# Shorter expert blocks under two conditions in a row, and a hint for each branch on the way to the next block

## The chip, the cores and the metric

The kernel runs on one core of one Trainium2 chip. The metric is the device time of one execution in microseconds (us); of several runs the median is taken. One of the executions was also recorded by the hardware profiler, and everything said about single instructions comes from that record. The core has five engines that each run their own instruction stream: TensorE (PE, matrix products, with the weight loads listed apart as PEld), VectorE (DVE), ScalarE (ACT), GpSimd (POOL) and SyncE (SP, which here only issues transfers). [...]

## The reference

The network has two layers over 1250 tokens (nodes) of 512 features: in each a graph part, an attention-like mixer and a feed-forward part with a router. The change touches only the last stage, the feed-forward part of the second layer: a layer norm, a router that picks two of eight experts for every token, an expert of 512 to 2048 to 512 with an exact GELU between, and the sum of the two experts' results weighted by their gates.

```python
    def _L1_ffn_ref(x, ln_g, ln_b, w_r, b_r, W1, b1, W2, b2):
        E = 8
        K = 2
        ...
        logits = jnp.einsum('btd,ed->bte', h, w_r) + b_r
        topk_vals, topk_idx = jax.lax.top_k(logits, K)
        gates = jax.nn.softmax(topk_vals, axis=-1)
        hf = h.reshape(B * T, d)
        hid = jax.nn.gelu(jnp.einsum('nd,edf->nef', hf, W1) + b1, approximate=False)
        expert_stack = jnp.einsum('nef,efd->ned', hid, W2) + b2
        ...
        mixed = jnp.sum(gathered * gates_flat[:, :, None], axis=1).reshape(B, T, d)
        return x + mixed
    ...
    x = x + _L1_ffn_ref(_layernorm(x, axis=-1)[None], ...)[0]
```

The reference computes every expert for every token and gathers afterwards. The kernel computes only the pairs of token and expert that the router picked, 2500 of them, so how much work each expert has is known only once the router's result is there.

## The kernel before, in words

**Before the experts.** The graph parts, the mixers, the first layer's feed-forward part and the second router take the first 830 us or so. At their end the kernel has sorted the 2500 pairs by expert, has turned the tokens' features into columns in that order (`hts`, 128 features x slots, four chunks of features), and holds for each slot the row of the output that it belongs to (`to_row`) and its gate (`to_gate`). A small table `plan` says for each expert where its slots start (`first`), how many blocks of 256 slots it fills (`full`), what is left over beside them (`part`: 0 for nothing, 1 for a block of 128, 2 for a block of 192) and its first column in `to_row` and `to_gate` (`col`).

**One block.** `block` (from L1355) runs an expert on 128, 192 or 256 slots. `hidden` makes the 16 chunks (`FC`) of the hidden layer: for each chunk four matmuls (L1306, weights `w1s`, one for each chunk of features) and a GELU on ACT (L1309) that writes `hid[f]`. For 128 and 256 slots `result` follows: for each 128 slots 16 matmuls with `hid[f]` as the weights and `w2s` as the moving data (L1329, 512 columns), one for the bias (L1331), and then `add_rows`: DVE scales by the gates (L1318) and POOL issues an indirect transfer that adds the rows into the output (L1319). For 192 slots `result_192` computes the transposed product, four chunks `c` of 16 matmuls of 192 columns each (L1344, bias L1346), copied out by DVE and turned back by eight transposes (L1352). The data of these matmuls is 32 bits wide, and each stands in the trace as two instructions (32 rows of L1329 for the 16, 0.43 us apart at full clock), the transposes as one.

**The order of the experts.** A Python loop over the eight experts writes the program for all of them out. In it, for expert e: `load_weights` makes SP issue weights of a later expert; `plan_of(e + 1)` loads the next expert's four numbers into registers of every engine (L1386), one expert ahead; then come the conditions, each a compare-and-branch on every engine: is there a shorter block (`part > 0`, L1399); is it 128 wide (`part == 1`, L1400, label `one{e}`), with the 192-wide block as its Else; then the blocks of 256, up to five (`MB`), nested into one another (L1366, label `full{e}_{b}`: is `full > b`).

**What each branch jumps over.** Code is laid out with the "true" arm behind the branch (`preferred_fallthrough_block`), so a true condition goes straight on, and a false one jumps past the block: past 268 recorded matmuls and as many weight loads for a 192-wide one, 161 for a 128-wide one, 194 for each of the five nested blocks of 256. After a 128-wide block there is a jump, without a condition, past the Else, the 192-wide block; it has L1400 as its line. Where a path skips a block, its arm holds the semaphore updates and waits which keep the engines' counts the same on both paths.

**Hints.** `mark_branch_hint_location` puts an instruction into TensorE's stream that tells its sequencer, ahead of a labelled branch, which way it will go; the value is computed in registers (one for "goes straight on", zero for "jumps"). There are two to each block, made by the function `ahead_of` and placed among the last matmuls of the block: in `result` at the last 128 slots' f = 10 and f = 13 (L1327, L1328), in `result_192` at the last chunk's f = 0 and f = 8 (L1342, L1343). The first hints the next L1366 of the same expert, the second the next expert's L1400. L1399 has no hint, and none of the other engines gets any.

**This data.** The router's result for these inputs gives the following blocks in order: expert 0: 128; expert 1: 192; expert 2: 128; expert 3: 192, 256; expert 4: 256; expert 5: 128, 256, 256; expert 6: 192; expert 7: 128, 256, 256, 256. This is read off the widths of TensorE's matmuls in the trace.

SP's order in this stage is written out by hand (`manual_schedule`): its weight loads stand where the loop puts them.

Of the kernel before, what the change touches and what calls it, by code (L numbers as in the profile page):

```python
# [23 lines left out]
DC = D // 128  # L24
# [18 lines left out]
FC = F1 // 128  # L43
FG = F1 // D
NB = (2 * N + 127) // 128
MB = (N + 63) // 256
# [24 lines left out]
def gps_two_layer_kernel(ctx: ExitStack, tc: tile.TileContext, x, src, dst, ew, rows, cols,  # L71
# [1053 lines left out]
    with tc.tile_pool(name="moe", bufs=1) as ep:  # L1125
# [171 lines left out]
        with tc.tile_pool(name="ox", bufs=3) as ox, \  # L1297
# [24 lines left out]
            def result(e, col, width, ahead):  # L1322

                for s in range(width // 128):
                    pm = po.tile([128, D], F32, name="po")
                    for f in range(FC):
                        if s == width // 128 - 1 and f in (FC - 6, FC - 3):  # L1327
                            ahead(f == FC - 6)  # L1328
                        nc.tensor.matmul(pm, hid[f][:, s * 128:(s + 1) * 128], w2s[e, f // DC][:, f % DC, :],  # L1329
                                         start=(f == 0), stop=False)  # L1330
                    nc.tensor.matmul(pm, row_pick[:, e:e + 1].to_broadcast([96, 128]), b2_parts,  # L1331
                                     start=False, stop=True)
                    add_rows(pm, col + s, 128)

            def result_192(e, col, ahead):

                turned = ox.tile([128, DC, 192], F32, name="turned", bufs=1)
                for c in range(DC):
                    pm = po.tile([128, D], F32, name="po")
                    chunk = slice(c * 128, (c + 1) * 128)  # L1340
                    for f in range(FC):
                        if c == DC - 1 and f in (0, FC // 2):  # L1342
                            ahead(f == 0)  # L1343
                        nc.tensor.matmul(pm[:, :192], w2s[e, f // DC][:, f % DC, chunk], hid[f][:, :192],  # L1344
                                         start=(f == 0), stop=False)
                    nc.tensor.matmul(pm[:, :192], b2_parts[:, chunk], row_pick[:, e:e + 1].to_broadcast([96, 192]),  # L1346
                                     start=False, stop=True)
                    nc.vector.tensor_copy(turned[:, c, :], pm[:, :192])
                for s, n in ((0, 128), (1, 64)):
                    pr = po.tile([128, D], F32, name="po")  # L1350
                    for c in range(DC):
                        nc.tensor.transpose(pr[:n, c * 128:(c + 1) * 128], turned[:, c, s * 128:s * 128 + n], ident)  # L1352
                    add_rows(pr, col + s, n)
# [18 lines left out]

                tc.mark_branch_hint_location(f"full{e}_{b}", (plan_e[1] + (7 - b)) // 8, [mybir.EngineType.PE])

            def ahead_of(e, plan_e, b):

                def hint(first):
                    if first and b < MB:
                        fetch_ahead(e, plan_e, b)
                    elif not first and e + 1 in plans:  # L1380
                        tc.mark_branch_hint_location(f"one{e + 1}", (3 - plans[e + 1][2]) // 2,
                                                     [mybir.EngineType.PE])
                return hint

            def plan_of(e):
# [6 lines left out]
            with tc.manual_schedule(engines={mybir.EngineType.SP}):  # L1392
                plans = {0: plan_of(0)}
                for e in range(E1):
                    load_weights(2 * FG * (e + 2))
                    plan_e = plans.pop(e)
                    if e + 1 < E1:
                        plans[e + 1] = plan_of(e + 1)
                    with tc.If(plan_e[2] > 0, preferred_fallthrough_block=True):  # L1399
                        with tc.If(plan_e[2] == 1, label=f"one{e}", preferred_fallthrough_block=True) as one:  # L1400
                            block(e, plan_e, plan_e[1], 128, ahead_of(e, plan_e, 0))
                        with one.Else():
                            block(e, plan_e, plan_e[1], 192, ahead_of(e, plan_e, 0))
                    blocks_of_256(e, plan_e, 0)

# [46 lines left out]
```

## Time and profile before

| what | value |
|---|---|
| runs of the kernel before | median 1511.21 us, 3 runs, 1510.18 to 1511.75 |
| the profiled execution | 1508.84 us, of it 1507.1 us span from first to last instruction |
| mean granted TensorE clock over the span | 0.966 |
| TensorE busy, 0 to 830 us | 750.25 us of 830 |
| TensorE busy, 830 to 1045 us | 200.43 us of 215 |
| TensorE busy, 1045 to 1260 us | 204.08 us of 215 |
| TensorE busy, 1260 to 1500 us | 237.70 us of 240 |
| DVE, ACT, POOL busy, 830 to 1500 us | 25.0, 110.3, 35.6 us |
| instructions fetched for TensorE over the span (queue q8) | 82 packets, 1.34 MB |

The 830 us and the other limits are cuts for the table, near the start of the experts and between two blocks. The experts' stage lasts from there to about 1500 us, and in it the other engines are idle most of the time. The biggest groups of TensorE in it, with busy time, mean duration of one, and the idle time before them with what ended it (`big` and `w` are names of the same weight buffers, pooled):

```profile
L1329 PE MATMUL po<-w,big 128*128 128x512 f32 x576 | 250.1, 592 | 0.0
L1306 PE MATMUL pm<-hts,big 128*128 x960 | 183.3, 353 | 14.8 <-issue 13.5 <-DVE o L1318 1.0 <-PE po L1352 0.3
L1306 PE MATMUL pm<-hts,w 128*128 x832 | 143.5, 334 | 13.8 <-PEq L1399 5.9 <-issue 5.7 <-DMA big<-in_w_dram 2.2
```

"Issue" is time in which the engine waited for nothing that the profile shows, and "PEq" is TensorE's sequencer. All idle time of the two groups of L1306 together is 28.6 us, and it lies in front of the first matmul of a block.

The sequencer's records can be listed by line as well: a compare-and-branch, a load of registers or a semaphore wait with its start and duration. A branch that goes wrong for the instruction fetch shows as one that lasts microseconds.

### The profile page before, as it was taken

What the parts mean: (1) busy time and instruction counts of PE and PEld (TensorE: products, weight loads), DVE (VectorE), ACT (ScalarE), POOL (GpSimd) and SP (SyncE); (2) the same over time, 40 slices, a digit from 0 to 9 for tenths busy, and PEclk for the clock granted to TensorE, in tenths of its full rate; (3) what the DMA queues carried; (4) which work ended last, traced back from release to release, by engine and by line L of the source; (5) the groups of instructions that cost most, each with busy time, mean ns of one, the idle gap of its engine ahead of it and who ended that gap; (6) DMA issues with size and microseconds to landing.
All of it is one profiled execution on the core that took longest, in us unless ns stands there. A gap on an engine that the chain in (4) does not pass through costs nothing. (4 is left out here: it accounts for less than half of the span.)

```text
span 1507.1 us, 18469 instructions
## 1 busy us (share of the span) xinstructions
PE 1392.5 (92%) x6082; PEld 871.0 (58%) x6082; DVE 586.0 (39%) x1425; ACT 404.9 (27%) x937; POOL 199.3 (13%) x176
## 2 busy tenths in 40 slices
PE   5999999999999699999965899899999999999997
PEld 3444445434554346554544697794767577975673
DVE  8887777699775673344476000000000000000000
ACT  8655445301223413112223221210212012110110
POOL 3345445400000000000005000000000000000000
PEclk9999999999999899999986999899999999999999
DMA  7312111522510030001149466600643006101011
GB/s 225 99 55 62 56 55 49 178 83 89 172 48 14 31 131 3 0 1 36 47 152 349 149 222 236 227 9 11 230 125 115 13 3 215 36 6 14 1 14 15
DMA packets 72766, 134.75 MB, mean 89 GB/s; under 512 B 8328, under 2 KB 9720, under 8 KB 72622
## 3 DMA queue, kind: packets, MB, share of 16 engines
q1 hardware_dynamic: 67694, 122.47, 24.0%
q0 software_dynamic: 4928, 10.43, 3.5%
q8 instruction: 82, 1.34, 0.4%
q14 instruction: 62, 0.51, 0.1%
HBM read 107.27 MB, written 26.38 MB: 89 GB/s over the span
## 5 line engine op out<-in xcount | busy, mean ns | idle before, releaser
L1329 PE MATMUL po<-w,big 128*128 128x512 f32 x576 | 250.1, 592 | 0.0
L1306 PE MATMUL pm<-hts,big 128*128 x960 | 183.3, 353 | 14.8 <-issue 13.5
L1318 DVE TENSOR_SCALAR o<-po,to_gate 128x512 f32<-128x512 f32 (+1 forms) x24 | 17.7, 749 | 452.9 <-PE po L1331 451.6
L1306 PEld LDWEIGHTS pm<-hts,big 128*128 128x128 f32 x960 | 165.8, 194 | 34.4 <-issue 19.0
L1329 PEld LDWEIGHTS po<-w,big 128*128 128x128 f32 x576 | 109.1, 190 | 132.1 <-issue 131.5
L1309 ACT ACTIVATE big<-pm,cols_sb 128x256 f32<-128x256 f32 (+2 forms) x224 | 96.2, 433 | 282.5 <-PE pm L1306 281.8
L1306 PE MATMUL pm<-hts,w 128*128 x832 | 143.5, 334 | 13.8 <-PEq L1399 5.9
L1306 PEld LDWEIGHTS pm<-hts,w 128*128 128x128 f32 x832 | 132.1, 197 | 24.6 <-issue 15.6
L455 PE MATMUL pm<-big,ht 128*125 128x512 f32 x240 | 130.9, 633 | 0.0
L1319 POOL DMA_INDIRECT out_dram<-o,row x24 | 37.0, 1540 | 645.2 <-DVE o L1318 284.2
L429 DVE TENSOR_TENSOR at<-at,pa 128x160 f32 x320 | 102.2, 319 | 41.3 <-PE pa L427 17.7
L400 POOL TENSOR_TENSOR hm<-hm,w_low 125x640 bf16<-125x640 bf16 x80 | 100.4, 1276 | 114.0 <-DVE hm L394 63.3
L123 PE MATMUL pm<-w,at 128*125 128x512 f32 x240 | 114.2, 598 | 0.0
L397 ACT ACTIVATE hm<-hm,w_top 125x80 bf16<-125x80 bf16 x320 | 86.4, 350 | 68.1 <-DVE hm L394 55.1
L633 PE MATMUL pn<-big,at 125*125 125x512 f32 x200 | 89.5, 605 | 3.0 <-DMA big<-q_d 3.0
L455 PE MATMUL pm<-big,xt 128*125 128x512 f32 x160 | 88.8, 646 | 1.2 <-DMA x_t<-in_x_dram 1.2
L1309 ACT ACT_TABLE_LOAD x11 | 14.1, 1283 | 248.9 <-PE pm L1306 248.9
L427 PEld LDWEIGHTS <-hs 125*128 125x128 bf16 x640 | 50.8, 97 | 48.8 <-issue 44.0
L424 PE MATMUL pa<-hm,hs 125*128 125x160 bf16 x320 | 64.6, 233 | 13.0 <-DVE at L429 10.9
L424 PEld LDWEIGHTS <-hs 125*128 125x128 bf16 x320 | 31.1, 97 | 67.8 <-issue 38.6
L633 PEld LDWEIGHTS pn<-big,at 125*125 125x125 f32 x200 | 37.5, 190 | 52.7 <-issue 52.7
L427 PE MATMUL pa<-hm,hs 125*128 125x80 bf16 x640 | 64.4, 198 | 0.0
(391 smaller groups left out, 1622.2 us busy)
## 6 DMA issues: line engine op xcount, KB each, us to landing
w<-in_w_dram SPq DMA_DIRECT2D x52, 1024.0 KB
big<-in_w_dram SPq DMA_DIRECT2D x12, 1024.0 KB
x_t<-in_x_dram SPq DMA_DIRECT2D x10, 224.0 KB
xn_d<-xr SPq DMA_DIRECT2D x10, 224.0 KB
y_d<-o SPq DMA_DIRECT2D x10, 224.0 KB
z_d<-o SPq DMA_DIRECT2D x10, 224.0 KB
q_d<-o SPq DMA_DIRECT2D x10, 224.0 KB
k_d<-o SPq DMA_DIRECT2D x10, 224.0 KB
```

Source lines behind the costliest of these rows:

```text
L123: nc.tensor.matmul(ps, lhs[:, c, :], w[:, c, :], start=(c == 0), stop=(row is None and c == DC - 1))
L397: nc.scalar.activation(hm[:, j, 1, :], hm[:, j, 0, :], AF.Copy, scale=w_top[:, g * J + j:g * J + j + 1])
L400: nc.gpsimd.tensor_tensor(hm[:, :, 2 + i, :], hm[:, :, 0, :], w_low[:, i, c8, None].to_broadcast([CH, J, TW]), ALU.mult)
L424: nc.tensor.matmul(pa.rearrange("p k c -> p (k c)"), hs[:, j, :], hm[:, j, 0:2, :].rearrange("p k c -> p (k c)"), start=True, stop=False)
L427: nc.tensor.matmul(pa[:, 1, :], hs[:, j, :], hm[:, j, 2 + i, :], start=False, stop=(i == 1))
L429: add = nc.vector.tensor_tensor(to, to, pa.rearrange("p k (t w) -> p k t w", t=T), ALU.add)
L455: nc.tensor.matmul(pm, lhs[:, c, :], w_sb[:, c, :], start=(c == 0), stop=(row is None and c == DC - 1))
L633: nc.tensor.matmul(pn, at[:P, 0, s, t * P:(t + 1) * P], y[:, s, :], start=(s == 0), stop=(s == T - 1))
L1306: nc.tensor.matmul(pm[:, :width], w1s[e, f // DC][:, c, (f % DC) * 128:(f % DC + 1) * 128], hts[:, c, bass.ds(start, width)], start=(c == ...
L1309: nc.scalar.activation(hid[f][:, :width], pm[:, :width], AF.Gelu, bias=cols_sb[:, C_B11 + e * FC + f:C_B11 + e * FC + f + 1])
L1319: nc.gpsimd.indirect_dma_start(out, bass.IndirectOffsetOnAxis(ap=row[:n], axis=0), o[:n], None, bounds_check=N - 1, oob_is_err=False, comp ...
L1329: nc.tensor.matmul(pm, hid[f][:, s * 128:(s + 1) * 128], w2s[e, f // DC][:, f % DC, :], start=(f == 0), stop=False)
```

## The change

In place of a condition with an Else there are two conditions one after the other, `part == 1` (label `one{e}`) and `part == 2` (label `two{e}`), both inside `part > 0`, which gets the label `any{e}`. After a 128-wide block the jump past the 192-wide one becomes the second condition, false in that case. Up to four hints go into each block in place of two, in the order of the branches that follow: `two` of the same expert (only in a 128-wide block), the next L1366, the next expert's `any`, the next expert's `one`. They stand at f = 10, 11, 12 and 13 of the last 128 slots in `result`, and at f = 0, 2, 4 and 6 of the last chunk in `result_192`. So the hint on L1366 moves by one f in the first and by two in the second, the hint on `one` stays at f = 13 in the first and moves from f = 8 to f = 6 in the second. What is computed stays the same. In the text of the prediction the lines keep their numbers of before; in the changed kernel the load of the plan is L1393, `any` L1406, `one` L1407, `two` L1409, and L1366 stays.

```diff
--- before.py
+++ after.py
@@ -1324,8 +1324,8 @@
                 for s in range(width // 128):
                     pm = po.tile([128, D], F32, name="po")
                     for f in range(FC):
-                        if s == width // 128 - 1 and f in (FC - 6, FC - 3):
-                            ahead(f == FC - 6)
+                        if s == width // 128 - 1 and f >= FC - 6:
+                            ahead(f - FC + 6)
                         nc.tensor.matmul(pm, hid[f][:, s * 128:(s + 1) * 128], w2s[e, f // DC][:, f % DC, :],
                                          start=(f == 0), stop=False)
                     nc.tensor.matmul(pm, row_pick[:, e:e + 1].to_broadcast([96, 128]), b2_parts,
@@ -1339,8 +1339,8 @@
                     pm = po.tile([128, D], F32, name="po")
                     chunk = slice(c * 128, (c + 1) * 128)
                     for f in range(FC):
-                        if c == DC - 1 and f in (0, FC // 2):
-                            ahead(f == 0)
+                        if c == DC - 1 and f % 2 == 0:
+                            ahead(f // 2)
                         nc.tensor.matmul(pm[:, :192], w2s[e, f // DC][:, f % DC, chunk], hid[f][:, :192],
                                          start=(f == 0), stop=False)
                     nc.tensor.matmul(pm[:, :192], b2_parts[:, chunk], row_pick[:, e:e + 1].to_broadcast([96, 192]),
@@ -1372,14 +1372,21 @@
 
                 tc.mark_branch_hint_location(f"full{e}_{b}", (plan_e[1] + (7 - b)) // 8, [mybir.EngineType.PE])
 
-            def ahead_of(e, plan_e, b):
-
-                def hint(first):
-                    if first and b < MB:
+            def ahead_of(e, plan_e, b, shorter=False):
+
+                on_pe = [mybir.EngineType.PE]
+
+                def hint(i):
+                    if i == 0 and shorter:
+                        tc.mark_branch_hint_location(f"two{e}", (plan_e[2] + 1) // 3, on_pe)
+                    elif i == 1 and b < MB:
                         fetch_ahead(e, plan_e, b)
-                    elif not first and e + 1 in plans:
-                        tc.mark_branch_hint_location(f"one{e + 1}", (3 - plans[e + 1][2]) // 2,
-                                                     [mybir.EngineType.PE])
+                    elif i in (2, 3) and e + 1 in plans:
+                        part = plans[e + 1][2]
+                        if i == 2:
+                            tc.mark_branch_hint_location(f"any{e + 1}", (part + 1) // 2, on_pe)
+                        else:
+                            tc.mark_branch_hint_location(f"one{e + 1}", (3 - part) // 2, on_pe)
                 return hint
 
             def plan_of(e):
@@ -1396,10 +1403,10 @@
                     plan_e = plans.pop(e)
                     if e + 1 < E1:
                         plans[e + 1] = plan_of(e + 1)
-                    with tc.If(plan_e[2] > 0, preferred_fallthrough_block=True):
-                        with tc.If(plan_e[2] == 1, label=f"one{e}", preferred_fallthrough_block=True) as one:
-                            block(e, plan_e, plan_e[1], 128, ahead_of(e, plan_e, 0))
-                        with one.Else():
+                    with tc.If(plan_e[2] > 0, label=f"any{e}", preferred_fallthrough_block=True):
+                        with tc.If(plan_e[2] == 1, label=f"one{e}", preferred_fallthrough_block=True):
+                            block(e, plan_e, plan_e[1], 128, ahead_of(e, plan_e, 0, True))
+                        with tc.If(plan_e[2] == 2, label=f"two{e}", preferred_fallthrough_block=True):
                             block(e, plan_e, plan_e[1], 192, ahead_of(e, plan_e, 0))
                     blocks_of_256(e, plan_e, 0)
```

## The prediction

> **What bounds the kernel now.** I read first the page's shares, then TensorE's timeline from 780 us on, then the sequencer's own records, line by line. TensorE is the bound:
>
> ```profile
> span 1507.1 us, 18469 instructions
> PE 1392.5 (92%) x6082; PEld 871.0 (58%) x6082; DVE 586.0 (39%) x1425; ACT 404.9 (27%) x937; POOL 199.3 (13%) x176
> ```
>
> The change touches only the experts, where TensorE stands still between blocks and hardly ever inside one. So the timeline's rows with a bracket (idle time before the row) are what can be won; the two rows without one, at 1145.37 and 1331.97, follow a 128-wide block with no idle time, and these are what can be lost:
>
> ```profile
> 865.21 17.52 PE L1306 MATMUL pm<-hts,big 128*128 x96 [4.19 <-issue]
> ...
> 912.35 16.16 PE L1306 MATMUL pm<-hts,w 128*128 x128 [2.20 <-DMA big<-in_w_dram]
> ...
> 949.47 18.44 PE L1306 MATMUL pm<-hts,big 128*128 x96 [7.01 <-issue]
> ...
> 1057.31 29.47 PE L1306 MATMUL pm<-hts,w 128*128 x128 [5.92 <-PEq L1399]
> ...
> 1145.37 20.88 PE L1306 MATMUL pm<-hts,big 128*128 x96
> ...
> 1259.30 21.06 PE L1306 MATMUL pm<-hts,w 128*128 x128 [2.70 <-issue]
> ...
> 1303.62 10.98 PE L1306 MATMUL pm<-hts,big 128*128 x96 [1.03 <-DVE o L1318]
> ...
> 1331.97 20.88 PE L1306 MATMUL pm<-hts,big 128*128 x96
> ```
>
> The sequencer's records (count: shortest/median/longest ns, first and last start) say what fills a gap. L1400 holds the jump that leaves a shorter block and the condition "is it 128 wide"; L1366 is "another block of 256", L1399 "any shorter block", L1386 the load of the plan:
>
> ```profile
> L1400 PEldq COMPARE_BRANCH  x1: 3372/3372/3372, 853.4 to 853.4; - x1
> L1366 PEldq COMPARE_BRANCH  x1: 4699/4699/4699, 856.8 to 856.8; - x1
> L1400 PEldq COMPARE_BRANCH  x1: 1772/1772/1772, 863.0 to 863.0; - x1
> L1366 PEldq COMPARE_BRANCH  x1: 3330/3330/3330, 1043.7 to 1043.7; - x1
> L1366 PEldq EVENT_SEMAPHORE  x1: 51/51/51, 1051.4 to 1051.4; - x1
> L1386 PEldq TENSOR_LOAD <-plan x1: 997/997/997, 1051.9 to 1051.9; - x1
> L1399 PEldq COMPARE_BRANCH  x1: 3532/3532/3532, 1053.0 to 1053.0; - x1
> L1400 PEldq COMPARE_BRANCH  x1: 6155/6155/6155, 1137.9 to 1137.9; - x1
> L1400 PEldq COMPARE_BRANCH  x1: 446/446/446, 1258.3 to 1258.3; - x1
> L1366 PEldq COMPARE_BRANCH  x1: 374/374/374, 1302.3 to 1302.3; - x1
> ```
>
> Three things are to be seen. First, prices: a branch not taken or taken nearby is 65 to 204 ns, a far one whose code is there 360 to 465, one whose code is not there 3.3 to 6.2 us. Second, cover: the jump at 1137.9 takes 6.2 us and the next matmuls start at 1145.37 without a gap, because the sequencer issues ahead (the jump starts 7.5 us before; after a 192-wide block only some 0.6). Third, where cover ends: at 1043.7 the far branch lasts until 1047.1, but the next record is a semaphore wait at 1051.4, just when the last matmul ends (1051.00+0.38). The path past a block that is skipped waits until TensorE has finished; all behind it is seen in full: in the 5.92 us gap the 1.0 us load and the 3.5 us miss.
>
> **The change part by part.** *Two conditions in a row.* The jump over the 192-wide block (268 matmuls and as many weight loads) after a 128-wide one becomes a short jump plus the condition "is it 192", far when it is false. Its arm for "false" holds, in the compiled order, a wait for TensorE's own count: that count includes all matmuls of the 128-wide block just issued. So the new far branch itself stays covered (3.4 to 6.2 us against 7.5 us), but everything behind it now starts at the drain.
>
> a) 128-wide to 256-wide (experts 5 and 7): gap 0 before. After the drain come the wait and a short jump (1051.4 to 1051.9 in the row above, 0.5 us), L1366 not taken (0.1), and 0.5 us from a branch to the first weight load (1056.75 to 1057.28 in the 5.92 us gap). +1.1 us each, +2.2. The nearest whole row, the 1.03 us gap, says the same. Bounds: 0.9 to 1.5.
>
> b) 128-wide to the next expert's 192-wide (experts 0 to 1, 2 to 3): before, jump and L1366 missed (3.4+4.7, and 6.1+4.9 at 934.8), 7.5 us of it covered, leaving 4.19 and 7.01. After: 0.5 until L1366, then L1366 either 0.4 (its hint held) or 3.4 (missed, now uncovered); wait and load 1.3; L1399 0.1; L1400 with its target fetched since the landing 1.2 to 1.8 (863.0 and 947.7), some 1.6; the added condition 0.3; to the load 0.6. That is 7.8 missed, 4.8 held. Missed: +3.6 and +0.8, sum +4.4. Held: +0.6 and -2.2, sum -1.6. Which one is the disputed point, below.
>
> c) Into a 192-wide block past the false "128" (expert 6, the 2.70 gap): one more wait and a branch not taken, +0.3 us.
>
> *More hints.* L1399 gets a hint. It is taken once, at expert 4, for 3532 ns; with its code there it costs about 0.45 (row 446). -3.1 us at the 5.92 gap. The hint stands in both blocks of expert 3, some 12 us ahead of the branch by the old hint's 1040.7; the wait at 1051.4 gives the fetch time. Bounds: 0 (hint lost) to -3.5 (nothing left).
>
> The hints themselves: each is two to three sequencer records (28 to 49 ns for the hint, 73 to 99 for the arithmetic), two more in most blocks, three in a 128-wide one. They stand among matmuls of 0.43 us, or 0.16 in a 192-wide block, with the sequencer ahead by the cover named. Zero; without that cover some 0.3 us each over about 30 hints, 9 us, but no row shows the sequencer late in front of a block's last matmuls.
>
> *Moved.* The hint on L1366 moves one of f later in 128- and 256-wide blocks (0.9 us), two of f in 192-wide ones (0.65 us of about 9). In the 192-wide blocks of experts 1 and 6 it worked (360 and 374 ns); one instruction fetch was recorded between 900 and 909 us, right after the hint at 901.0. 8.2 us remain against the 3.4 of a miss: zero. If it failed, 3.0 us each are seen.
>
> *Other engines.* ACT, DVE, POOL and SP pass the same extra condition. Their arms wait for their own work alone, POOL's for its own scatter (4.6 us to landing in the chain). ACT's last GELU ends 14 us before the drain, DVE's next output is 40 us away, and POOL's scatter waits for DVE. SP issues a skipped expert's weights at the same points of TensorE. Zero; in the worst case POOL is late by 5 us once per expert where it has 14.
>
> [...] The row: a branch over the 192-wide block takes 3.3 to 6.2 us. [...]
>
> **The disputed point: how many hints last.** Far L1366 with another jump-hint 2.7 us after it: 4699, 4863 (expert 2) and 3447 (expert 5). With a hint after it that expects no jump, or none: 360, 374, 465, 2083 and 3330. So a later jump-hint seems to replace the earlier one. After the change the 128-wide block hints "192", L1366, L1399 and L1400 within 2.6 us, and for experts 0 and 2 the last expects a jump. I take the miss. Against that: in the old path a missed jump lay between hint and branch, which may be what lost the hint.
>
> **Sum.** (a) +2.2, (b) +4.4, (c) +0.3, L1399 -3.1: +3.8 us. Against the profiled execution (span 1507.1, 1508.84 us with what lies around it) that is 1512.6; the median of the runs is 2.4 us above that execution, so the forecast is 1511.2+3.8 = 1515.0 us, slower by 0.25%.
>
> **The rivals.** *Hints last separately.* Both L1366 hit: +2.2-1.6+0.3-3.1 = -2.2, 1509.0 us. For it: the hit rows with a second hint behind them. If L1400 is also ready (446), 1.2 less at each of two places: -4.6, 1506.6 us, the case on the faster side: it decides if both L1366 stay under 0.5 us and L1400 under 0.5.
>
> *The new hint on L1399 is lost too*, to the hint behind it, which expects no jump. Then the 3.5 us remains: +6.9, 1518.1 us. For it: 3330 at 1043.7, where the hint behind expected none. Against: 2083, where it was the same.
>
> *It all hides.* The new drain costs nothing, since the old gaps held it: 1508 to 1511. Against: the two gaps of zero.
>
> **How the numbers follow.** Forecast 45%, L1399 lost too (or L1366 in a 192-wide block) 17%, hints separate without L1400 22%, with it 13%, hidden 3%. What a measurement of this kernel can tell is about 0.2%, 3 us. The forecast lies 0.8 us above that bound and its terms may be off by 1.5, so three tenths of it count as no change (slower 0.32); hints that last separately lie 0.8 us short of the bound on the other side, so four tenths of their 0.22 count as faster (0.09), and a third of the hidden case (0.01). Faster 0.13+0.09+0.01 = 0.23; slower 0.32+0.17 = 0.49; the rest, 0.28, no change. The range runs from the separate hints with L1400 to a lost L1399, 1506.5 to 1519.0. The forecast alone: 1513.5 to 1516.5.
>
> **What would show it.** Right: gaps of about 1.1 us in front of the 256-wide blocks of experts 5 and 7; a semaphore record at the end of TensorE's work after each 128-wide block; L1366 over 3 us behind it for experts 0 and 2, gaps near 7.8; L1399 under 0.5 us and expert 4's gap near 2.8. Wrong: L1366 near 0.4 there, or gaps that stay at zero. Time lost inside blocks would show the hints as not free.

## The result and the profile after

The changed kernel takes 1531.51 us (median of 4 runs, 1530.42 to 1534.31) where the kernel before takes 1511.48 us (4 runs of the same comparison): ratio 1.0136, 95% interval 1.0118 to 1.0154, so some 20 us more. The forecast was 1515.0 us, its range ended at 1519.0. The direction was right, the size was not.

The profiled execution of the changed kernel is its slowest of the four (1534.31 us, span 1532.5 us), that of before lay 2.6 us under its median; between these two traces 25.4 us have to be found. The page's head first, then TensorE's timeline from 850 us on, rows with idle time before them (without one of 0.28 us):

```profile
span 1532.5 us, 18587 instructions
...
PE 1401.2 (91%) x6082; PEld 876.3 (57%) x6082; DVE 584.9 (38%) x1425; ACT 405.1 (26%) x937; POOL 199.1 (13%) x176
```

```profile
870.35 18.84 PE L1306 MATMUL pm<-hts,big 128*128 x96 [8.01 <-DVE row L1316]
...
922.63 16.93 PE L1306 MATMUL pm<-hts,w 128*128 x128 [6.01 <-DMA big<-in_w_dram]
...
961.52 17.66 PE L1306 MATMUL pm<-hts,big 128*128 x96 [8.01 <-DVE row L1316]
...
1068.61 3.75 PE L1306 MATMUL pm<-hts,w 128*128 x8 [5.96 <-PEq L1406]
1073.63 28.24 PE L1306 MATMUL pm<-hts,w 128*128 x120 [1.27 <-issue]
...
1132.16 12.60 PE L1306 MATMUL pm<-hts,big 128*128 x96 [2.39 <-issue]
...
1163.29 20.96 PE L1306 MATMUL pm<-hts,big 128*128 x96 [1.01 <-DVEq L1409]
...
1277.58 21.07 PE L1306 MATMUL pm<-hts,w 128*128 x128 [2.98 <-DVEq L1407]
...
1324.96 13.57 PE L1306 MATMUL pm<-hts,big 128*128 x96 [4.10 <-PEq L1366]
...
1357.05 20.96 PE L1306 MATMUL pm<-hts,big 128*128 x96 [0.99 <-DVEq L1409]
```

The releaser named in a bracket is often not the one (DVE and a transfer of weights stand at gaps that TensorE's own branches fill); the sequencer's records tell it. Same columns as before (count, shortest/median/longest ns, first and last start); L1409 is the new condition "192", L1406 "any shorter block", L1366 "another block of 256":

```profile
L1409 PEldq EVENT_SEMAPHORE  x1: 51/51/51, 862.4 to 862.4; - x1
L1366 PEldq COMPARE_BRANCH  x1: 3562/3562/3562, 862.8 to 862.8; - x1
...
L1366 PEldq COMPARE_BRANCH  x1: 3413/3413/3413, 916.3 to 916.3; - x1
...
L1406 PEldq COMPARE_BRANCH  x1: 3566/3566/3566, 1064.3 to 1064.3; - x1
...
L1409 PEldq EVENT_SEMAPHORE  x1: 51/51/51, 1162.3 to 1162.3; - x1
...
L1366 PEldq COMPARE_BRANCH  x1: 3332/3332/3332, 1320.7 to 1320.7; - x1
```

The wait at 862.4 starts when the last matmul of expert 0's block ends (861.96 + 0.38), as foreseen, and L1366 behind it is missed in full view. New are the two L1366 at 916.3 and 1320.7, behind 192-wide blocks: 0.36 and 0.37 us before. L1406, hinted now, is as long as it was without a hint (3532 ns).

The hints themselves stand in the trace too, as records of the sequencer (with the line L1448 before and L1455 after). In expert 1's 192-wide block, first before, then after:

```profile
L1448 PEldq BRANCH_PREFETCH_HINT  x2: 35/42/49, 901.0 to 903.7; - x2
...
L1455 PEldq BRANCH_PREFETCH_HINT  x3: 28/35/49, 908.1 to 909.5; - x3
```

Before, an instruction fetch of 16 KiB (what one fetch brings is called a page here) starts 1.0 us after the first of these hints, and the next hint comes 2.7 us after it. After, the three hints stand 0.64 and 0.76 us apart, and no instruction fetch at all starts between the first of them and the branch:

```profile
DMA packets 0, 0.00 MB, mean 0 GB/s; under 512 B 0, under 2 KB 0, under 8 KB 0
```

That is the view of transfers from 908.1 to 916.3 us.

| place | gap before | gap after | forecast |
|---|---|---|---|
| expert 0 to 1 (128, then 192 wide) | 4.19 | 8.01 | 7.8 |
| expert 1 to 2 (192, then 128) | 2.20 | 6.01 | 2.2 |
| expert 2 to 3 (128, then 192) | 7.01 | 8.01 | 7.8 |
| expert 3 to 4 (256, then 256), and the gap 8 matmuls on | 5.92 | 5.96 + 1.27 | 2.8 |
| expert 5, 128 to 256 | 0 | 1.01 | 1.1 |
| expert 5 to 6 (256, then 192) | 2.70 | 2.98 | 3.0 |
| expert 6 to 7 (192, then 128) | 1.03 | 4.10 | 1.0 |
| expert 7, 128 to 256 | 0 | 0.99 | 1.1 |

All gaps from expert 0's end on, with two more that hardly change (0.28 and 2.29 us before, 0.28 and 2.39 after), come to 25.6 us before and 41.0 us after: 15.4 us of the 25.4. The second part is in no gap. The chunks of the hidden layer after a gap (L1306) take longer: the first row of expert 7's 13.57 us instead of 10.98, of expert 5's 12.60 instead of 11.03, all of expert 4's 31.99 without its inner gap instead of 29.47; over all blocks 8.0 us. The view by windows shows why. Its columns are the stretch, its length, the busy time of PE, PEld, DVE, ACT and POOL, the granted TensorE clock, the share of the transfer engines and GB/s; the first 4.8 us of expert 7, before and after:

```profile
1303.60:1308.40 4.80, 4.78 (x42) 4.80 (x43) 0.21 (x1) 2.54 (x5) 1.55 (x1) 1.00 0.43 56
...
1325.00:1329.80 4.80, 4.80 (x23) 4.80 (x24) 0.00 (x0) 2.02 (x3) 1.25 (x1) 0.50 0.25 41
```

Behind 4.10 us without work the clock is 0.50 and 23 matmuls are started where 42 were. The length of the gap does not decide alone: behind 2.29 us (expert 5 before) the clock stayed at 1.00, behind 2.39 us (expert 5 after) it fell to 0.50 for 3.41 us, behind 2.98 us (expert 6 after) it stayed at 1.00. Between 855 and 1495 us of these two traces, before and after, every stretch at 0.50 lasts one, two or three times 3.41 us. Cut the two traces into windows of that length, laid so that the clock changes at their edges, and the cases sort themselves. Two pairs of windows from expert 5 and expert 6 after:

```profile
1129.06:1132.47 3.41, 1.02 (x6) 0.34 (x3) 0.75 (x1) 0.00 (x0) 1.55 (x1) 1.00 0.00 0
1132.47:1135.88 3.41, 3.41 (x19) 3.41 (x18) 0.00 (x0) 1.78 (x3) 0.00 (x0) 0.50 0.91 195
...
1275.83:1279.24 3.41, 1.67 (x10) 1.70 (x11) 0.15 (x1) 0.05 (x1) 1.38 (x1) 1.00 0.49 63
1279.24:1282.65 3.41, 3.41 (x23) 3.41 (x22) 0.15 (x1) 2.38 (x4) 0.00 (x0) 1.00 1.04 369
```

The 2.39 us fall into one window, and the next one is at half the clock; the 2.98 us are divided over two, 1.23 and 1.75 us, and nothing happens. In that part of the two traces, a window at full clock with up to 1.95 us without work is followed by full clock, and each of the ten with 1.97 us or more by 0.50; out of 0.50, a window with up to 0.15 us without work leads back to 1.00, and one with 0.71 or more does not. The rest of the 25.4 us is 1.5 us by which the experts start later, 0.2 us at the end, and 0.3 us that no row shows.

### The profile page after: what moved, and what is told of

Its sections match the earlier page's. It is cut to its first block, busy times and chain, and to the rows that moved or that the text cites. A ratio compares the mean times of both kernels' runs of the same rounds, so it can differ in the third digit from the quotient of the medians.

```text
span 1532.5 us, 18587 instructions
## 1 busy us (share of the span) xinstructions
PE 1401.2 (91%) x6082; PEld 876.3 (57%) x6082; DVE 584.9 (38%) x1425; ACT 405.1 (26%) x937; POOL 199.1 (13%) x176
## 5 line engine op out<-in xcount | busy, mean ns | idle before, releaser
L1306 PE MATMUL pm<-hts,big 128*128 x960 | 188.2, 360 | 24.8 <-DVE row L1316 16.0
L1306 PEld LDWEIGHTS pm<-hts,big 128*128 128x128 f32 x960 | 170.3, 200 | 45.0 <-issue 29.6
L1306 PE MATMUL pm<-hts,w 128*128 x832 | 146.6, 339 | 19.1 <-DMA big<-in_w_dram 6.0
L1306 PEld LDWEIGHTS pm<-hts,w 128*128 128x128 f32 x832 | 134.0, 200 | 31.1 <-issue 21.6
L424 PE MATMUL pa<-hm,hs 125*128 125x160 bf16 x320 | 64.6, 233 | 12.9 <-DVE at L429 10.9
```

The costliest lines, as they stand in the source:

```text
L424: nc.tensor.matmul(pa.rearrange("p k c -> p (k c)"), hs[:, j, :], hm[:, j, 0:2, :].rearrange("p k c -> p (k c)"), start=True, stop=False)
L1306: nc.tensor.matmul(pm[:, :width], w1s[e, f // DC][:, c, (f % DC) * 128:(f % DC + 1) * 128], hts[:, c, bass.ds(start, width)], start=(c == ...
```

## The experiments

All runs are compared with the kernel before on the same chip (its medians there: 1508.70 to 1510.17 us). "Held" is a branch under 0.5 us, "lost" one over 3.3 us. `any`, `one` and `two` stand for the branches with these labels, L1366 for "another block of 256"; "f" counts the 16 matmuls among which the hints stand.

| kernel | time, us | ratio to before (95% interval) |
|---|---|---|
| two conditions, old hints | 1516.42 | 1.0050 (1.0033 to 1.0066) |
| Else, new hints | 1520.32 | 1.0082 (1.0066 to 1.0099) |
| changed, no hint on `one` | 1531.76 | 1.0156 (1.0136 to 1.0177) |
| before, `any` in place of `one` | 1510.68 | 1.0013 (0.9998 to 1.0027) |
| changed, 192-wide hints far apart | 1524.70 | 1.0108 (1.0086 to 1.0130) |
| before, 192-wide hints later | 1508.97 | 0.9996 (0.9985 to 1.0008) |
| before, 192-wide hints close | 1514.05 | 1.0030 (1.0020 to 1.0040) |
| before, `any` in 256-wide blocks | 1506.69 | 0.9987 (0.9975 to 0.9998) |
| changed, 192-wide hints as before | 1524.36 | 1.0101 (1.0078 to 1.0124) |
| changed, no hint on `two` | 1527.55 | 1.0111 (1.0090 to 1.0132) |
| changed, once more (one run) | 1529.83 | |
| before, `one` then `any` in 256-wide blocks | 1508.97 | 0.9997 (0.9984 to 1.0010) |
| before, code moved by 150 | 1518.88 | 1.0069 (1.0047 to 1.0090) |
| before, code moved by 256 | 1512.25 | 1.0029 (1.0012 to 1.0045) |
| changed, far apart, code moved by 190 | 1520.29 | 1.0084 (1.0065 to 1.0103) |
| changed, L1366 hinted last in 192-wide blocks | 1519.92 | 1.0072 (1.0054 to 1.0091) |

**The two halves of the change.** First the conditions alone, on the changed kernel:

```diff
-                        if s == width // 128 - 1 and f >= FC - 6:
-                            ahead(f - FC + 6)
+                        if s == width // 128 - 1 and f in (FC - 6, FC - 3):
+                            ahead(1 if f == FC - 6 else 3)
...
-                        if c == DC - 1 and f % 2 == 0:
-                            ahead(f // 2)
+                        if c == DC - 1 and f in (0, FC // 2):
+                            ahead(1 if f == 0 else 3)
```

> The two conditions in a row, with the two hints of before at their old places. Theory A (the extra hints lose the hint on L1366 in a 192-wide block): the gaps in front of experts 2 and 7 are those of before (2.2 and 1.0 us), the ones that the new wait makes stay as in the changed kernel (8.0 in front of experts 1 and 3, 1.0 in front of the 256-wide blocks of experts 5 and 7, 3.0 in front of expert 6), and expert 4's stays 5.9: some 7 us of gaps over before and up to 3 of slower blocks behind them, 1518 to 1522 us. Theory B (not the hints but where the code now lies loses it): 6.0 and 4.1 us in front of experts 2 and 7 as in the changed kernel, and about 1531 us.

1516.42 us, 7.0 us over before in the same comparison. Both branches behind the 192-wide blocks are held:

```profile
L1366 PEldq COMPARE_BRANCH  x1: 342/342/342, 912.6 to 912.6; - x1
...
L1366 PEldq COMPARE_BRANCH  x1: 359/359/359, 1307.9 to 1307.9; - x1
```

The gaps are 8.09, 2.09, 7.92, 6.01 and 0.99, 3.04, 1.00, 1.09 us at the places of the table above (without a second gap in expert 4), 7.2 us more in sum than before. Theory A holds, B falls in this form: the two conditions cost what the new wait costs, and the two branches are not lost without the other half. That half alone, on the changed kernel:

```diff
-                        with tc.If(plan_e[2] == 1, label=f"one{e}", preferred_fallthrough_block=True):
-                            block(e, plan_e, plan_e[1], 128, ahead_of(e, plan_e, 0, True))
-                        with tc.If(plan_e[2] == 2, label=f"two{e}", preferred_fallthrough_block=True):
+                        with tc.If(plan_e[2] == 1, label=f"one{e}", preferred_fallthrough_block=True) as one:
+                            block(e, plan_e, plan_e[1], 128, ahead_of(e, plan_e, 0))
+                        with one.Else():
```

> The Else of before, with the three hints L1366, any, one at the places of the changed kernel. Theory A (extra hints lose the one on L1366): the far branch of L1366 in front of experts 2 and 7 takes 3.3 to 3.4 us, the gaps are 5.2 to 6.0 and 4.1 us; no semaphore wait behind the 128-wide blocks and gaps of 4.2, 7.0, 0 and 0 us as before; any still 3.5 us at expert 4; 1518 to 1522 us. Theory B (place of the code): 0.36 us, 2.2 and 1.0 us, and 1511 us.

1520.32 us, 10.9 over before; no wait behind the 128-wide blocks, and L1366 lost in front of expert 2, but held in front of expert 7:

```profile
L1366 PEldq COMPARE_BRANCH  x1: 3365/3365/3365, 908.7 to 908.7; - x1
...
L1366 PEldq COMPARE_BRANCH  x1: 355/355/355, 1306.9 to 1306.9; - x1
```

Theory A held for one of the two. The two halves' losses, 0.50% and 0.82%, come to 1.32% of the 1.36% together, but not by the same places: the trace of this half has 4.5 us more of gaps than before, 1.46 us of them inside expert 7's block, and 4.4 us more in L1306 by the slow clock. That the sum fits so well is in part chance.

**Which hint counts.** From the changed kernel the hint on `one` is taken out, and in the kernel before it is replaced by one on `any`:

```diff
-                    elif i in (2, 3) and e + 1 in plans:
+                    elif i == 2 and e + 1 in plans:
```

> The changed kernel without the hint on one, so that the one on any is the last. Theory C (only the last hint counts): the branch any of expert 4 takes under 0.5 us in place of 3.6 and its gap falls from 6.0 to about 2.8 us; the branch one of expert 6, 0.45 us with its hint, takes up to 3.4 us; L1366 in front of experts 2 and 7 stays at 3.4 us, since a hint still follows it by 0.64 us. About the time of the changed kernel, 1529 to 1533 us. Theory D (a hint on a branch whose page is not there does nothing): any stays 3.5 us, one stays 0.45 us, and the time too.

`any` of expert 4 takes 0.43 us and its gap is 2.82 us; `one` of expert 6 takes 3.83 us (gap 6.32), and the gaps in front of experts 1 and 3 grow to 10.47 and 9.61, since the hint on `one`, the last one there too, is gone. What is won at one place is lost at three: 1531.76 us. Theory C.

```diff
                     elif not first and e + 1 in plans:
-                        tc.mark_branch_hint_location(f"one{e + 1}", (3 - plans[e + 1][2]) // 2,
+                        tc.mark_branch_hint_location(f"any{e + 1}", (plans[e + 1][2] + 1) // 2,
...
-                    with tc.If(plan_e[2] > 0, preferred_fallthrough_block=True):
+                    with tc.If(plan_e[2] > 0, label=f"any{e}", preferred_fallthrough_block=True):
```

> The kernel before with its second hint, at the same places, on any in place of one. Theory C (only the last hint counts, and 2.7 us are enough for the one before it to have fetched): any of expert 4 under 0.5 us, its gap 2.8 in place of 5.9; L1366 in front of experts 2 and 7 still 0.36 us; one of expert 6 up to 3.4 us in place of 0.45: 1509 to 1512 us. Theory D (a hint on a branch whose page is not there does nothing): nothing changes, 1511 us with 5.9 us in front of expert 4 and 0.45 us for one of expert 6. If any is held and one keeps its 0.45 us by itself: 1508 us.

`any` of expert 4: 0.42 us, gap 2.74; the branches behind the 192-wide blocks stay held (0.36 and 0.47); the gaps in front of experts 1 and 3 are 6.42 and 9.59 (4.19 and 7.01 before). 1510.68 us, no difference that can be told. `one` of expert 6 kept 0.44 us here, against theory C, with 0.90 us of waiting inside the block; in three other kernels in which `any` is the last hint it takes 3.4 to 3.8 us. Why not here stays open.

Over all traces: `any` of expert 4 is held in the four kernels in which its hint is the last one before its branch (gaps of 2.74 to 2.86 us), and lost, 3.4 to 3.8 us, in the seven in which a hint on `one` follows it.

**Distance and place in the 192-wide block.** On the kernel before, both hints two f later, or the second one close to the first:

```diff
-                        if c == DC - 1 and f in (0, FC // 2):
-                            ahead(f == 0)
+                        if c == DC - 1 and f in (2, 10):
+                            ahead(f == 2)
```

> The kernel before, both hints of a 192-wide block two f later (f = 2 and 10), their distance kept at 2.7 us. Theory E (distance): L1366 in front of experts 2 and 7 stays at 0.36 us and the time at that of before. Theory G (f = 2 is too late, or lies badly to the page of code): 3.4 us there, gaps of 5.8 and 4.1 us in place of 2.2 and 1.0, 1517 to 1520 us.

Both held (0.35 and 0.38 us), ratio 0.9996. Being two f later is not the cause. With `f in (0, 2)` and `ahead(f == 0)`:

> The kernel before, the first hint of a 192-wide block where it was (f = 0), the second one 0.65 us behind it (f = 2 in place of 8). Theory E (distance): L1366 in front of experts 2 and 7 takes 3.4 us at least at one of the two, 4 to 10 us over before. Theory G (place): 0.36 us at both, and the time of before.

L1366 takes 3.54 us in front of expert 2 and 0.37 in front of expert 7; 1514.05 us, 0.30% over before. The distance alone loses one of the two. On the changed kernel the distances are widened:

```diff
-                        if c == DC - 1 and f % 2 == 0:
-                            ahead(f // 2)
+                        if c == DC - 1 and f in (0, 8, 12):
+                            ahead({0: 1, 8: 2, 12: 3}[f])
```

> The changed kernel with the three hints of a 192-wide block at f = 0, 8 and 12, 2.7 and 1.3 us apart, in place of 0, 2, 4. Theory E (the hint on L1366 has to be alone for about 1 us, until its fetch has started): L1366 in front of experts 2 and 7 falls from 3.4 to 0.4 us, the gaps from 6.0 and 4.1 to 2.2 and 1.0, the blocks behind them start faster; 7 to 10 us less than the changed kernel, 1519 to 1523 us. Theory F (three hints are too many at any distance): both stay at 3.4 us and the time at 1529 to 1532.

Held in front of expert 2 (0.35 us), lost in front of expert 7 (3.41 us): neither theory. Nor does it help there to go back to the two hints of before in the 192-wide blocks (`f in (0, FC // 2)`, `ahead(1 if f == 0 else 3)`):

> The changed kernel, but the 192-wide blocks with the two hints of before (L1366 at f = 0, one at f = 8); the 128- and 256-wide blocks keep all of theirs. Theory E (in a 192-wide block it is the distance and number of the hints): L1366 in front of experts 2 and 7 0.36 us, gaps 2.2 and 1.0, and the time near that of the two conditions with the old hints, 1516 to 1520 us. If the hints of the other blocks cost something of their own: over 1522 us.

```profile
L1366 PEldq COMPARE_BRANCH  x1: 347/347/347, 911.6 to 911.6; - x1
...
L1366 PEldq COMPARE_BRANCH  x1: 3670/3670/3670, 1307.3 to 1307.3; - x1
```

1524.36 us, above what theory E allowed. These 192-wide blocks and conditions are those of the run with the old hints, which held both; all that differs are the hints in other blocks, and with them the place of the code. In these two traces with distant hints and expert 7's branch lost, no instruction fetch starts within 1.5 us of the hint in expert 6's block, and one starts 5.0 and 5.4 us after it, ahead of the branch; in the changed kernel it is 3.6 us. Eight such places show the mark. Where L1366 behind a 192-wide block is held, a fetch starts 1.0 to 1.3 us after its hint: before at both places, the two conditions with the old hints in front of expert 7, the code moved by 256 in front of expert 2. Where it is lost, none starts in that time: the first comes 3.6 and 5.4 us after the hint in front of expert 7 (the changed kernel, and the 192-wide hints as before) and 3.6 us after it in front of expert 2 with the code moved by 150; in front of expert 2 in the changed kernel, with the next hint 0.64 us behind, none comes before the branch.

**Is a loss chance?** The changed kernel was profiled once more, and run without the hint on `two` (the lines of `i == 0 and shorter` taken out):

> The changed kernel once more, to see whether the same hints are lost. If the code alone decides: 3.3 to 3.6 us at L1366 in front of experts 1, 2, 3 and 7, at any of expert 4, and 0.44 us at L1366 behind expert 4, as in the first trace. If chance has a part: at least one of these differs, and the span by 3 us or more with it.

> The changed kernel without the hint on two. Theory J (it does nothing: the branch follows too soon, its miss is covered by the matmuls already issued): two still takes 3.4 to 4 us at experts 0, 2, 5 and 7, gaps 8.0, 8.0, 1.0 and 1.0 us, time of the changed kernel, 1529 to 1533 us. Theory K (it takes the place of the hint on L1366): L1366 behind the 128-wide blocks of experts 0 and 2 falls to 0.4 us, gaps near 5, 6 us less.

The second trace has the same hits and losses: L1366 3.42, 3.31, 3.57, 3.70 us in front of experts 1, 2, 3 and 7, `any` 3.37, L1366 behind expert 4 0.44; span 1528.1. In these two traces of one code, the code decides. Without its hint, `two` takes 3.4 to 4.4 us as with it (3.5 to 4.0), under cover, and L1366 behind it 3.6 and 3.7: theory J. The time, 1527.55, is 1.5 us under the expected band, with overlapping intervals.

**The place of the code.** In the kernel before, small matmuls into an unused tile were put ahead of the first transposes, where TensorE waits 7.6 us; nothing else changes but that all code behind moves, by 150 instructions with 75 of them and by 256 with 128:

```diff
                 hg = rows_at.pop(b)
+                if b == 0:
+                    spare = ps.tile([128, DC, 128], F32, name="pg", tag="pg", bufs=4)
+                    for _ in range(75):
+                        nc.tensor.matmul(spare[:P, 0, :E1], ones_b, before[:, T, :], start=True, stop=True)
```

> The kernel before with 75 small extra matmuls (150 instructions) into an unused tile ahead of the first transposes, where TensorE waits 7.6 us anyway; all code of the experts moves by 150 instructions. Theory M (a hint is lost when a page of code ends between it and its branch): an instruction fetch between hint and branch, and L1366 at 3.3 to 3.8 us in place of 0.36 in front of experts 2 and 7, gaps 5.8 and 4.1, 7 to 11 us over before (besides up to 2 us of the extra matmuls). Theory N (place is nothing): 0.36 us and no change but the extra matmuls.

> The same with 128 extra matmuls, 256 instructions: the code lies to the pages as in the kernel before. Theory M: both hints held, 0.36 us and gaps of 2.2 and 1.0 as before; time of before plus what 128 small matmuls cost outside the 7.6 us wait, 0 to 6 us, seen as a later start of the experts.

L1366 is L1370 in these. Moved by 150, the two branches behind the 192-wide blocks:

```profile
L1370 PEldq COMPARE_BRANCH  x1: 3867/3867/3867, 907.4 to 907.4; - x1
...
L1370 PEldq COMPARE_BRANCH  x1: 3617/3617/3617, 1305.9 to 1305.9; - x1
```

Moved by 256:

```profile
L1370 PEldq COMPARE_BRANCH  x1: 353/353/353, 911.9 to 911.9; - x1
...
L1370 PEldq COMPARE_BRANCH  x1: 364/364/364, 1305.3 to 1305.3; - x1
```

And the fetches between hint and branch of expert 1: the view of transfers, in 40 slices from the hint to the branch, first moved by 150 (898.5 to 907.4 us):

```profile
DMA  0000000000000000300000000000000000000000
...
q8 instruction: 1, 0.02, 0.8%
```

then moved by 256 (903 to 911.8 us):

```profile
DMA  0000030000000000000000000000000000000000
...
q8 instruction: 1, 0.02, 0.9%
```

In the second the one packet comes 1.2 us after the hint (slice 6 of 0.22 us) and can be the hinted one; in the first it comes 3.6 us after it (slice 17), and the branch fetches again, 1.5 us after its start. 1518.88 us against 1512.25. The place of the code is shown to decide here: the same hints are lost with the code moved by 150 instructions and held again with it moved by 256, as theory M has it. That the late fetch is the sequential one, of a page that ends between hint and branch, is the likely reading and not shown: the trace does not name what a packet holds, and in one kernel (`any` in place of `one`) a fetch also starts 5.0 us after the hint in expert 6's block, behind one at 1.15 us, and the branch is held. How much code one fetch brings can be estimated from the trace of before: between 44.4 and 285.2 us, without a branch of TensorE, 12 fetches of 16 KiB start, one for every 257 of its recorded instructions, and between 329.1 and 757.8 us 13, one for every 253. By this estimate a move by 256 is about one fetch; hints that were held are held again after it. What the move by 256 costs, 0.29%, is within what was expected for the extra matmuls; the traces don't put it at one place.

Then the same in the changed kernel, with the distant hints and 95 such matmuls (190 instructions), so that no fetch should fall between:

> The changed kernel with distant hints in the 192-wide blocks (f = 0, 8, 12) and 95 extra matmuls (190 instructions) ahead. Theory M: no fetch between hint and branch at experts 1 and 6, L1366 0.36 us at both, gaps 2.2 and 1.0: 4 to 6 us less than without the move, 1517 to 1521 us. Theory N: expert 7's stays at 3.4 us, 1524 us.

Both held (0.34 and 0.36 us), 1520.29 us against 1524.70 unmoved. And without moving, with the hint on L1366 last and late:

```diff
-                        if c == DC - 1 and f % 2 == 0:
-                            ahead(f // 2)
+                        if c == DC - 1 and f in (0, 6, 12):
+                            ahead({0: 2, 6: 3, 12: 1}[f])
```

> The changed kernel with the hints of a 192-wide block in the order any, one, L1366, at f = 0, 6 and 12. Theory C (the last hint is the one that counts): L1366 in front of experts 2 and 7 at most 1.5 us (its fetch may not be over when the branch comes), gaps under 3.5 and 2.3; 4 to 8 us less than the changed kernel. Theory F (three hints are too many): 3.4 us at both.

Both held (0.45 and 0.47 us) with three hints in the block: 1519.92 us, less than the changed kernel by more than the forecast of 4 to 8 us (1.0072 against 1.0136). Theory F falls.

**Something better than both?** The kernel before, with `any` hinted at the end of the 256-wide blocks alone, and `one` at the end of the shorter ones:

```diff
+                    elif not first and b and e + 1 in plans:
+                        tc.mark_branch_hint_location(f"any{e + 1}", (plans[e + 1][2] + 1) // 2,
+                                                     [mybir.EngineType.PE])
                     elif not first and e + 1 in plans:
...
-                    with tc.If(plan_e[2] > 0, preferred_fallthrough_block=True):
+                    with tc.If(plan_e[2] > 0, label=f"any{e}", preferred_fallthrough_block=True):
```

> The kernel before, where only the 256-wide blocks hint any in place of one as their second hint; the shorter blocks keep theirs. Theory C (the last hint is the one that counts): any of expert 4 0.43 us in place of 3.5, its gap 2.8 in place of 5.9; one in front of experts 1 and 3 as before (1.2 to 1.8 us, gaps 4.2 and 7.0), one of expert 6 still 0.44 us, with up to 0.9 us of waiting inside the block: 2 to 3 us under before. If what any wins is lost elsewhere (one of expert 6 at 3.4 us): no change.

```profile
L1402 PEldq COMPARE_BRANCH  x1: 367/367/367, 1049.9 to 1049.9; - x1
...
L1403 PEldq COMPARE_BRANCH  x1: 3504/3504/3504, 1250.4 to 1250.4; - x1
```

`any` (L1402) of expert 4 is held, `one` (L1403) of expert 6 lost: gap 2.81 in place of 5.92, and 5.74 in place of 2.70. The 1506.69 us, ratio 0.9987 with an interval that ends at 0.9998, are the best of all kernels here, but these two gaps do not explain them. In a last one the 256-wide blocks hint L1366 at f = 10, `one` at 12 and `any` at 14:

> As the version with any only in the 256-wide blocks, but there one is hinted too, 1.7 us ahead of any (L1366 at f = 10, one at 12, any at 14); shorter blocks hint L1366 and one at the old distance. Theory L (a hint that expects no jump displaces nothing): any of expert 4 0.4 us and one of expert 6 0.45 us, gaps 2.8 and 2.7, 1503 to 1505 us. Theory C (the last hint counts, whichever way): any 0.4, one of expert 6 3.4 to 3.8 us with a gap near 5.8, 1506 to 1508 us.

`one` of expert 6 is lost again (3.41 us, gap 5.70), though it had been hinted 1.6 us ahead of `any`. The hint on `any` expects no jump there, as the one on `one` behind expert 3 does: such a hint displaced another here too. 0.9997.

## Why the prediction was wrong

**Right, with its size.** (a) 1.01 and 0.99 us in front of the 256-wide blocks of experts 5 and 7, forecast 1.1, with the wait for TensorE's end as named. (b) 8.01 and 8.01 where 7.8 was said; the disputed point went as chosen, L1366 behind the 128-wide blocks missed at 3.4 to 3.6 us once TensorE had finished. (c) +0.28, forecast +0.3. The conditions alone were measured at 7.0 us; the forecast's terms for them, (a) to (c), were 6.9.

The reason given for the disputed point, a later hint that expects a jump, is not what the runs show: L1366 is missed there as well where the last hint expects no jump (3.54 and 3.40 us without the hint on `one`). So the outcome was right and the reason not, which is luck. No run has this L1366 held, with two hints or with four. The text's other thought, that a missed jump between hint and branch loses the hint, stays untested, since `two`, or the jump in its place, is missed in every run.

**The step that failed** is "Moved", the hint on L1366 in the 192-wide blocks: "zero. If it failed, 3.0 us each are seen." It failed at both places, for 3.8 and 3.1 us. The argument counted only the time left for the fetch. In front of expert 2 the next hint follows after 0.64 us, and in the changed kernel's trace the fetch never starts: the branch is lost in each of the five kernels, one of them traced twice, where the distance is 0.63 to 0.75 us, and held in all where it is 2.6 us or more, or where no hint follows, except in the one moved by 150 instructions. In front of expert 7 the place of the longer code is enough: without a move it is lost at distances of 2.6 and 2.7 us too, and held there with the code moved by 190. The end of a page between hint and branch is the likely reason, not shown. Close hints without a fetch between were held there in two kernels and lost in one, so the distance does not decide alone. What else does stays open.

**The second** is the 3.1 us that L1399, now L1406, was to win. It was lost to the hint on `one` 1.0 us behind it, which expects no jump: the rival with 17%. The text had counted such a hint as harmless from rows that were held; the two of them with such a hint behind them, 360 and 374 ns, had their fetch begun 1.0 and 1.1 us after the hint, and the next hint came at 2.7 us. The range ended where one of these hints is lost; three were.

**The term that was missing** is the clock. The forecast took each block at its old length. Gaps over 4 us, and some of 2 to 3, are followed by some 3 to 6 us at half the clock, and 9 at expert 4: 8.0 us of the 25.4. The old trace had it, behind the gaps in front of experts 1, 2, 3 and 4 (0.50 to 0.66 over some 4.8 us), and it wasn't charged to the gaps. Expert 4's 1.27 us in mid-block was not foreseen either; it comes 8 matmuls after a missed branch, ends 2.6 us after the start of an instruction fetch (1071.1), and also stands in the second trace of this kernel (1.54 us). Its cause stays open.

In sum: forecast +3.8; the two lost hints +6.9, `any` not won +3.1, expert 4's inner gap +1.3, small differences +0.3: 15.4 us of gaps. With 8.0 of clock and 1.7 outside the experts it is 25.1 of the 25.4 between the two traces, of which 5.4 are the distance of these two executions from their medians.

The hints themselves (28 to 49 ns each) cost nothing that shows, as said: TensorE stands still at none of them.

## What to carry to other kernels

Do not take a branch hint as kept because it was given: here a hint that followed could displace it, also one that expects no jump. `any` of expert 4 was held in 4 of 4 kernels with its hint last and in none of 7 with another 1.0 us behind it. The safest reading is one hint per stretch, for the branch that costs most, with nothing behind it, though no run here tries that throughout. Whether a hint took can be read from the trace: for L1366 behind a 192-wide block, a fetch started 1.0 to 1.3 us after the hint at the four places read out above where the branch was short, and at none of the four where it was long. A hint that worked, worked for a place of the code: with 150 instructions more ahead, the branch in front of expert 2 took 3.87 us in place of 0.36; after a change ahead of it, read every far branch's duration again. Price a new gap of TensorE by its length and by the slow clock behind it, which here added half as much again (8.0 us to 15.4).

## What was not expected of the hardware

The same code, moved by 150 instructions, ran 0.69% slower than the kernel before, moved by 256 0.29% (both with the extra matmuls). Which of the hints on L1366 in the 256-wide blocks are held (0.43 to 0.47 us in some kernels, 1.6 to 2.1 or 3.3 to 3.9 in others) follows none of the rules above: some are held with the next hint 0.8 us behind them, and some are lost with it 2.8 us behind; it costs nothing, since the sequencer is there some 7 us ahead of the matmuls.
